# A two-layer graph attention network on one core: another order of work for the last, short node tile

## The chip, the cores and the metric

The kernel runs on one core of one Trainium2 chip. The metric is the device time of one execution, in microseconds (us). Engines go by the profile's names: PE multiplies matrices (PEld is its weight load), DVE and ACT work element by element, POOL issues the gathers, SP and ACT issue plain DMA transfers. PSUM is the memory that PE writes its products into; SBUF is the on-chip memory of everything else.

## The reference

A residual block on 3125 nodes of 768 features with 53,125 directed edges (25,000 drawn pairs in both directions, and a self loop for each node), sorted by destination. Cut to what matters:

```python
h0 = relu(layernorm(x))                                  # no gain, no bias
h = gat(h0, W1, heads=4, out=256, concat)                # 1024 wide
h1 = relu(layer_norm(h, g1, be1)) + h0 @ Wr1 + br1
h = gat(h1, W2, heads=1, out=768)
out = x + layer_norm(h, g2, be2) + h1 @ Wr2 + br2

def gat(h, W, a_src, a_dst, bias):                       # per head
    xl = h @ W
    e = leaky_relu((xl @ a_src)[src] + (xl @ a_dst)[dst], 0.2)
    e = exp(e - segment_max(e, dst)[dst])
    alpha = e / (segment_sum(e, dst)[dst] + 1e-16)
    return segment_sum(xl[src] * alpha, dst) + bias
```

All of it is float32. A graph whose edge list is not in the form above is handled by a second program behind a branch (`any_order`), which does not run here.

## The kernel before

The nodes are cut into NB = 25 tiles of 128 rows, which are the destinations of the sums. The last, tile 24, has only 53 rows (`LAST`). The edges of a tile lie in 17 slots of 128 (`J`), those of tile 24 in 8 (`JL`). A slot covers one or two quarters of a tile's destinations (32 rows each), so the sum of a slot is a matmul whose output is 32 rows: its weights are the attention weights of 128 edges (128 x 32), its moving operand is the 128 gathered source rows. The slots of a tile are taken in five rounds (`ROUNDS`). A float32 matmul shows as two records in the profile.

**Stages.** (1) x is normalised and transposed, and `product(b, i)` (L853 to L872) multiplies each tile by W1 and the folded attention vectors: 1032 columns in three steps of C = 344, six matmuls a step. ACT copies each step out of PSUM into `row`, and the row is stored to `table1` in DRAM (L870); the attention scores go to `asad1`. Beside it runs other work (`beside`), and after each pair of matmul groups the loop takes steps of it. (2) Source scores are looked up for each edge slot, and the layer-1 softmax is made. (3) `sums` (L655) gathers the rows of `table1` by POOL's indirect DMA (L197, L201) and sums them by PE (L757). When a tile's last round is issued, its `finish` is added to a list `running`; every later round takes one step of each member of that list (`step`). `finish` reads the sum out of PSUM (for the first tiles after some rounds of waiting), and goes on into `end1` (L1151 to L1204), which does the bias, the layer norm (L498 statistics, L502 square root on ACT, L1166 normalisation), the transposes on PE (L1173, `flip`), ReLU and gain on ACT (L1178, `turn`), the residual's addition on DVE (L1180), the product with W2 (L1195 by `dense`: L182 for a tile of 128 rows, L186 for one of 53), the copies of that product by ACT (L1201) and DVE (L1203), and the store of the row to `table2` (L218). The products h0 @ Wr1 for some tiles are made in `later`, by the same `pr` buffers in PSUM, which are two, as are the `p2` buffers that transposes and W2 products share. (4) Layer 2 goes through the same tiles: for tile b the five rounds of `summed` (L1379) run while the softmax of tile b + 1 is prepared: `values` (L1322: ACT spreads one gathered column over 32 lanes of `slots`), `softmax` (L1333; transposes into `mix` L1340, maximum L1343, exponentials L1349 and L1350, transposes back L1354, weights copied by DVE L1357 and ACT L1358), `totals2` (L1403 to L1407). `finish` (L1384) adds the tile's own share to the sum in `pa` (L1392), scales it by the softmax's total and adds the bias (L1396), normalises (L1399, L1400) and stores. The product h1 @ Wr2 fills PE between the rounds (`residuals`). `pa` and `mix` have one PSUM buffer each in layer 2.

**`dense`** (L179) is a matmul that for a tile of fewer than 128 rows is cut into pieces of 32 output rows, which take different columns of the array; `half_at` (L188) gives the rows of PSUM for a half of the output columns, so that the two halves of a 53-row tile lie side by side: rows 0 to 52 and 64 to 116.

**What sets the order.** In layer 1's sums and in layer 2 the instructions of PE, ACT and DVE keep the order in which the code issues them (`manual_schedule`); the generators' `yield`s decide it. SP and POOL issue what is left in the order that the framework gives them, each transfer waiting for its buffer and its data. A buffer with a name and a count (`bufs`) is waited for when the same name comes round.

**Names in this text.** `own` is the row of a node itself (its self loop); `v` holds, per node, the sum of exponentials, the self loop's exponential, twice that (v2) and the reciprocal of the total (v3); `xr` is x plus the second residual; `z` is the row that is normalised; `h1` holds a tile's transposed layer-1 result.

## Time and profile before

| What | Value |
|---|---|
| three runs | 1892.24, 1896.75, 1896.78 us |
| median | 1896.75 us |
| profiled execution, own time | 1885.98 us |
| its span | 1884.1 us |
| mean granted clock of PE | 0.966 |
| busy: PE, weight loads, DVE | 1720.1 (91%), 939.4 (50%), 1000.9 us (53%) |
| busy: POOL, ACT | 906.1 (48%), 446.4 us (24%) |
| moved | 541.28 MB, mean 287 GB/s |

The profile is of one execution, and its time lies below the three others. The span runs from the first to the last instruction. In the page's chain of work that ended last, PE has 24% of the span, and DVE, DMA and the rest a few per cent each; the stages are better read one by one. The DMA's row over 40 slices reads 7 and 8 tenths in the first two, 2 to 5 (once 8) until the 11th, 9 from the 12th to the 25th, 4 in the 26th, and 8 to 9 from there to the last but one. The granted clock's row is at 9 almost throughout, with an 8 in the 12th, 27th, 35th and 39th slice and a 7 in the last.

### The profile page before, as it was taken

How to read it: one execution, taken by the hardware profiler on the slowest of the kernel's cores; microseconds unless marked ns; L12 is line 12 of the kernel's file. 1: busy time of each engine (PE TensorE's matmuls, PEld its weight loads, DVE VectorE, ACT ScalarE, POOL GpSimd, SP SyncE). 2: the span in 40 equal slices, each digit the busy share in tenths (PEclk: the TensorE clock that was granted, in tenths of full speed). 3: DMA queues.
4: the chain of work that ended last, by engine and by line, in shares of the span. 5: the costliest groups of instructions: out<-in, count | busy, mean ns of one | idle time of the engine just before them, and what ended most of it. 6: DMA issues, size and time to landing. Idle time of an engine off the chain costs nothing. (4 is left out here: it accounts for less than half of the span.)

```text
span 1884.1 us, 31010 instructions
## 1 busy us (share of the span) xinstructions
PE 1720.1 (91%) x11411; PEld 939.4 (50%) x11411; DVE 1000.9 (53%) x2641; ACT 446.4 (24%) x1286; POOL 906.1 (48%) x922
## 2 busy tenths in 40 slices
PE   8999999999889999999999998969778989889884
PEld 5666665566456555565555544433333334333331
DVE  7673433888845556656655655412434434244435
ACT  2122331000212211221221211222323333233232
POOL 2000102000256666666666666166666666666662
PEclk9999999999989999999999999989999999899987
DMA  7824538432399999999999999499899899999883
GB/s 231 292 83 143 144 88 286 138 129 94 135 383 373 384 384 373 387 368 389 372 367 378 364 362 362 168 373 312 301 323 331 317 328 321 330 335 323 293 295 130
DMA packets 173672, 541.28 MB, mean 287 GB/s; under 512 B 32963, under 2 KB 58329, under 8 KB 173384
## 3 DMA queue, kind: packets, MB, share of 16 engines
q0 software_dynamic: 100912, 381.56, 55.9%
q1 hardware_dynamic: 68206, 147.26, 22.7%
q10 hardware_dynamic: 4394, 10.39, 1.4%
q8 instruction: 93, 1.52, 0.3%
q14 instruction: 67, 0.55, 0.1%
HBM read 498.62 MB, written 65.62 MB: 299 GB/s over the span
## 5 line engine op out<-in xcount | busy, mean ns | idle before, releaser
L197 POOL DMA_INDIRECT g<-table,idx_s x409 | 414.7, 1014 | 406.0 <-DVE al L606 174.8
L201 POOL DMA_INDIRECT g<-table,hi_s x423 | 434.7, 1028 | 239.9 <-issue 88.8
L1379 PE MATMUL pa<-g,w 128*32 128x384 f32 x1956 | 239.4, 520 | 62.7 <-issue 33.2
L182 PE MATMUL pr<-wr,h 128*128 128x384 f32 x768 | 283.0, 508 | 2.1 <-issue 2.1
L757 PE MATMUL pa<-g,w 128*32 128x256 f32 x3912 | 255.8, 387 | 15.7 <-issue 10.1
L182 PE MATMUL p<-w,h1T 128*128 128x384 f32 (+1 forms) x768 | 267.4, 496 | 0.0
L182 PEld LDWEIGHTS pr<-wr,h 128*128 128x128 f32 x768 | 141.4, 196 | 126.5 <-issue 58.5
L182 PEld LDWEIGHTS p<-w,h1T 128*128 128x128 f32 x768 | 139.9, 189 | 113.2 <-issue 21.8
L757 PEld LDWEIGHTS pa<-g,w 128*32 128x32 f32 x3912 | 122.3, 110 | 141.5 <-issue 50.7
L1379 PEld LDWEIGHTS pa<-g,w 128*32 128x32 f32 x1956 | 62.8, 113 | 215.9 <-issue 175.7
L734 DVE TENSOR_TENSOR w<-oh,al 128x128 f32<-128x128 f32 (+1 forms) x416 | 131.9, 317 | 61.5 <-PE pa L757 21.7
L1343 DVE CUSTOM_DVE_ANT_0 e<-mix,pen 128x640 f32<-128x640 f32 x25 | 20.6, 825 | 262.9 <-PE mix L1340 125.8
L182 PE MATMUL pr<-h0k,wr 128*128 128x256 f32 (+1 forms) x576 | 143.9, 395 | 1.1 <-issue 0.9
L862 PE MATMUL pm<-w,h0l 128*128 128x344 f32 (+1 forms) x468 | 142.5, 459 | 0.0
L999 PE MATMUL pm<-h0g,wr 128*128 128x512 f32 x288 | 132.8, 608 | 0.0
L862 PE MATMUL pm<-w,h0g 128*128 128x344 f32 x432 | 130.3, 457 | 0.3 <-ACT h0g L841 0.3
L182 PEld LDWEIGHTS pr<-h0k,wr 128*128 128x128 f32 x576 | 106.7, 192 | 33.2 <-issue 14.4
L930 POOL DMA_DIRECT2D hot_d<-ohd x25 | 13.4, 538 | 221.0 <-DVE own L513 123.7
L733 DVE TENSOR_SCALAR oh<-iota_f,rel_s 128x32 f32<-128x32 f32 (+1 forms) x416 | 114.0, 274 | 0.5 <-issue 0.3
L862 PEld LDWEIGHTS pm<-w,h0l 128*128 128x128 f32 (+1 forms) x468 | 85.7, 187 | 44.9 <-issue 7.1
L862 PEld LDWEIGHTS pm<-w,h0g 128*128 128x128 f32 x432 | 81.6, 192 | 40.5 <-issue 1.2
L1322 ACT ACTIVATE slots<-g 128x32 f32<-128x32 f32 x416 | 66.8, 219 | 131.9 <-DMA g<-table,idx_s 91.1
(288 smaller groups left out, 1671.1 us busy)
## 6 DMA issues: line engine op xcount, KB each, us to landing
s<-slo_d SPq DMA_DIRECT2D x25, 544.0 KB
table<-row SPq DMA_DIRECT2D x24, 512.0 KB
own<-table SPq DMA_DIRECT2D x24, 512.0 KB
h1T_d<-h1T SPq DMA_DIRECT2D x24, 512.0 KB
h<-h1T_d SPq DMA_DIRECT2D x22, 512.0 KB
table<-row SPq DMA_DIRECT2D x24, 392.0 KB
ring<-in_x_dram SPq DMA_DIRECT2D x24, 384.0 KB
xr<-in_x_dram SPq DMA_DIRECT2D x24, 384.0 KB
```

What stands on the lines that cost most here:

```text
L182: nc.tensor.matmul(out_, lhsT, rhs, start=start, stop=stop)
L197: nc.gpsimd.indirect_dma_start(out=g, out_offset=None, in_=table[:, :], in_offset=bass.IndirectOffsetOnAxis(ap=idx_s[:, c], axis=0))
L201: nc.gpsimd.indirect_dma_start(out=g, out_offset=None, in_=table[:, :], in_offset=bass.IndirectOffsetOnAxis(ap=idx_k[:, c], axis=0), bound ...
L733: nc.vector.tensor_scalar(oh, iota_f[:, lo:hi], rel_s[:, c:c + 1], None, op0=OP.is_equal)
L734: nc.vector.tensor_tensor(w, oh[:, None, :].to_broadcast([128, heads, hi - lo]), al[:, POS[j], :, b:b + 1].to_broadcast([128, heads, hi - ...
L757: nc.tensor.matmul(pa[p0:p0 + 32, o // f, o % f:o % f + n], w[:, o // cols, :], g[:, o:o + n], start=to not in opened, stop=False, skip_gr ...
L862: nc.tensor.matmul(pm[:r, :C], h0[b][:, k, :], w1[:, k, i * C:(i + 1) * C], start=(k == 0), stop=(k == NK1 - 1))
L930: nc.gpsimd.dma_start(hot_d[b], ohs[b])
L999: nc.tensor.matmul(pm, wr1[:, k, m * 128:(m + 1) * 128], groups[gi][:, k, :], start=(k == 0), stop=(k == NK1 - 1))
L1322: nc.scalar.activation(slots[b % 2][:, POS[j], :], gs[b, j][:, C2:C2 + 1].to_broadcast([128, 32]), AF.Copy)
L1343: nc.vector.tensor_tensor_reduce(out=e, in0=mix[:, :WIN], in1=pen, scale=1.0, scalar=-BIG, op0=OP.add, op1=OP.max, accum_out=top)
L1379: nc.tensor.matmul(pa[p0:p0 + 32, i, :f], w_, g[:, i * f:(i + 1) * f], start=(i, q) not in opened, stop=False, skip_group_check=True)
```

## The change

It touches the last tile (53 rows) in three places.

**A, `product`.** For the 53-row tile a step of 344 columns is cut into two halves of 172, which `dense` puts side by side: per step and per k four matmuls (two halves, each in pieces of 32 and 21 rows) in place of one of 344 columns. ACT copies each half on its own.

**B, the end of layer 1.** After the last tile's rounds the list `running` is turned round, so that in each step the members of later tiles are taken first: tile 24's `finish` ahead of tile 23's. The last tile's transposes go into a `pr` buffer in place of a `p2` buffer. Tile 23's loop over W2 yields twice more after the sixth of its eight steps.

**C, the end of layer 2.** In tile 23, ahead of its first round, the own rows of tile 24 are loaded, into a buffer of the `h1` kind; the rest of the values of tile 24 are spread and its softmax is begun. The weights and totals of tile 24 follow behind round 1 in place of round 4. A new function, `own_share`, has POOL multiply the own rows by v2 and v3 and add the bias b2 (two instructions). `finish` of tile 24 then computes z = pa * v3 + own, and leaves out the separate scaling and bias. The load of the own rows at the end of tile 23's `finish` is gone.

The diff, cut to its core:

```diff
@@ sums
             k = 0
+            running.reverse()
             while running:
@@ product
+                    parts = 1 if r == P else 2
+                    n = C // parts
                     for k in range(NK1):
-                        nc.tensor.matmul(pm[:r, :C], h0[b][:, k, :], w1[:, k, i * C:(i + 1) * C],
-                                         start=(k == 0), stop=(k == NK1 - 1))
+                        for h in range(parts):
+                            o = i * C + h * n
+                            dense(pm[:, :n], h0[b][:, k, :], w1[:, k, o:o + n], r,
+                                  start=(k == 0), stop=(k == NK1 - 1), at=half_at(b, h).start)
...
+                            for h in range(parts):
+                                o = i * C + h * n
+                                e = min(o + n, HC) - o
+                                at = half_at(b, h)
+                                nc.scalar.activation(row[:, o:o + e], pm[at, :e], AF.Copy)
...
@@ end1
-                    pt = pp.tile([128, 512], F32, name="p2", bufs=2).rearrange("p (k n) -> p k n", n=128)
+                    pt = pp.tile([128, 512], F32, name="pr" if b == NB - 1 else "p2", bufs=2).rearrange("p (k n) -> p k n", n=128)
...
                     if k in (2, 5):
                         yield
+                    if k == 5 and b == NB - 2:
+                        yield
+                        yield
@@ load_own
+                if b == NB - 1 and b not in owns:
+                    owns[b] = small([128, NK2, P], "h1", bufs=3).rearrange("p k n -> p (k n)")[:, :C2]
@@ finish, layer 2
+                if b < NB - 1:
+                    nc.vector.scalar_tensor_tensor(z[:, cs], own[:r, cs], v[:, 2:3], pa[half_at(b, i), i, :f],
+                                                   op0=OP.mult, op1=OP.add)
+                else:
+                    nc.vector.scalar_tensor_tensor(z[:, cs], pa[half_at(b, i), i, :f], v[:, 3:4], own[:r, cs],
+                                                   op0=OP.mult, op1=OP.add)
-            load_own(b + 1)
+            if b + 1 < NB - 1:
+                load_own(b + 1)
             yield
-            nc.vector.scalar_tensor_tensor(z, z, v[:, 3:4], b2_b[:r], op0=OP.mult, op1=OP.add)
+            if b < NB - 1:
+                nc.vector.scalar_tensor_tensor(z, z, v[:, 3:4], b2_b[:r], op0=OP.mult, op1=OP.add)
...
+        def own_share(b):
+            r = rows_of(b)
+            own, v = owns[b][:r], shares[b][1][:r]
+            nc.gpsimd.tensor_scalar(own, own, v[:, 2:3], v[:, 3:4], op0=OP.mult, op1=OP.mult)
+            nc.gpsimd.tensor_tensor(own, own, b2_b[:r], OP.add)
@@ layer 2's loop
+                last = b + 1 == NB - 1
                 for k in range(len(ROUNDS)):
+                    if last and k == 0:
+                        load_own(b + 1)
+                        for i in range(2, len(ROUNDS)):
+                            values(b + 1, i)
+                        made = softmax(b + 1)
+                        next(made)
                     summed(b, k, pa, opened)
...
-                    if b + 1 < NB:
+                    if b + 1 < NB and not last:
...
-                        if b + 1 < NB:
-                            next(made)
-                            next(made, None)
-                            totals2(b + 1)
+                    if b + 1 < NB and k == (1 if last else 4):
+                        next(made)
+                        next(made, None)
+                        totals2(b + 1)
+                        if last:
+                            own_share(b + 1)
```

What this does to the instructions is seen best in rows of the order, where each row is one instruction (or a run of like ones): line, operation, output, inputs, rows x columns. A number behind a name tells buffers apart.

DVE at the end of layer 1, before: rows of 53 are tile 24's, the copy of 128x2 takes tile 23's attention scores out of its W2 product.

```order
L498 BN_AGGR bn_mv<-bn_st 53x2
L1203 COPY asad_109<-p_11999 128x2
L506 RECIPROCAL bn_rs<-bn_sd 53x1
L1166 TENSOR_SCALAR z<-z,bn_mv,bn_rs 53x1024
L1180 TENSOR_TENSOR h1T<-h1T,r1l 128x4x53 x2
L1190 MEMSET row_12066 53x15
```

The same place on DVE now (lines below the first edit are 9 to 12 higher).

```order
L498 BN_AGGR bn_mv<-bn_st 53x2
L506 RECIPROCAL bn_rs<-bn_sd 53x1
L1175 TENSOR_SCALAR z<-z,bn_mv,bn_rs 53x1024
L1189 TENSOR_TENSOR h1T<-h1T,r1l 128x4x53 x2
L1215 COPY asad_109<-p_12056 128x2
L1199 MEMSET row_12123 53x15
```

Tile 23's copy stood between tile 24's statistics and its normalisation; it now stands behind tile 24's residual addition.

PE at the same place, before: the two `p` of 384 and 386 columns are tile 23's W2 product, `ident,z` are tile 24's transposes, and the pieces of 32 and 21 rows are its W2 product.

```order
L182 MATMUL p_11998<-w_4663,h1T 128x384
L182 MATMUL p_11999<-w_4663,h1T 128x386
L182 MATMUL p_11998<-w_4663,h1T 128x384
L182 MATMUL p_11999<-w_4663,h1T 128x386
L1173 MATMUL p_12045<-ident,z 128x53 x4
L1173 MATMUL p_12050<-ident,z 128x53 x4
L186 MATMUL p_12068<-w_4663,h1T 32x384
```

PE at the same place now.

```order
L1182 MATMUL pr<-ident,z 128x53 x8
L182 MATMUL p_12055<-w_4720,h1T 128x384
L182 MATMUL p_12056<-w_4720,h1T 128x386
L182 MATMUL p_12055<-w_4720,h1T 128x384
L182 MATMUL p_12056<-w_4720,h1T 128x386
L186 MATMUL p_12125<-w_4720,h1T 32x384
```

The eight transposes stand ahead of the last two of the eight steps of tile 23's product, and in the `pr` buffers.

ACT at the end of layer 2, before: the exponentials (e, then v) and the copy of 128x128 are of tile 24's softmax, the first store is tile 22's output, the square root of 128x1 is tile 23's.

```order
L1322 ACTIVATE slots_12124<-g_16096 128x32
L1349 ACT_TABLE_LOAD
L1349 ACTIVATE e,v<-e,top 128x640
L1350 ACTIVATE v<-self_s,top 128x1
L218 DMA out_dram<-z 128x768
L1358 ACTIVATE w<-mix 128x128
L502 ACT_TABLE_LOAD
L502 ACTIVATE bn_sd<-bn_mv,eps 128x1
```

The same place on ACT now; the first square root is tile 22's, the second tile 23's.

```order
L1336 ACTIVATE slots_12181<-g_16153 128x32
L1363 ACTIVATE e,v<-e,top 128x640
L1364 ACTIVATE v<-self_s,top 128x1
L502 ACT_TABLE_LOAD
L502 ACTIVATE bn_sd<-bn_mv,eps 128x1
L1372 ACTIVATE w<-mix 128x128
L218 DMA out_dram<-z 128x768
L502 ACTIVATE bn_sd<-bn_mv,eps 128x1
```

Tile 24's exponentials stand ahead of tile 22's square root, without a table load of their own, and the one table load that is left stands ahead of tile 22's square root; tile 23's needs none.

9 lines of the change are left out of this document (3 added, 6 removed).

## The prediction

> **What bounds the kernel now.** I read the table of windows first, because the kernel is a chain of stages with different limits, and then the timelines of all engines at the three places that the change touches: around 294 us, around 1200 us and from 1850 us to the end. Columns of the first fence: window, its length, busy time of PE, its weight loads, DVE, ACT and POOL, granted clock, DMA share, GB/s.
>
> ```profile
> 340.00:380.00 40.00, 40.00 (x367) 25.14 (x366) 35.53 (x77) 2.75 (x4) 0.00 (x0) 0.97 0.34 111
> 700.00:900.00 200.00, 198.94 (x1669) 117.93 (x1668) 122.09 (x401) 40.97 (x117) 132.45 (x132) 1.00 1.00 381
> 1300.00:1500.00 200.00, 170.87 (x950) 72.06 (x950) 78.97 (x164) 63.02 (x199) 131.21 (x131) 0.95 0.90 315
> ```
>
> Between the layers' gathers (340 to 380) PE has no gap and the DMA is two thirds idle: PE bounds it. In layer 1's sums (700 to 900) PE and the DMA are both full. In layer 2 (1300 to 1500) the DMA is at 0.90 and PE at 85%: gathers, PE and a clock a little below 1 share the limit. None of these long stretches is changed. What is changed are the joints between them, and a joint that ends earlier moves everything behind it, if what follows starts from that joint. So the three parts are costed one by one and the rest is taken to shift. (A measurement of this kernel can tell about 0.3%, 5.7 us, from no change.)
>
> **Part 1, the last tile's W1 product.** Timeline rows: start, length, engine, line, operation, operands, count, and in brackets the idle time before it and what ended it.
>
> ```profile
> 293.83 10.62 PE L862 MATMUL pm<-w,h0l 128*53 128x344 f32 x36
> 304.80 0.58 DVE L551 TENSOR_REDUCE own<-pd 128x136 f32<-128x408 f32 x1 [8.77 <-PE pd L545]
> 309.16 1.01 POOL L197 DMA_INDIRECT g<-table,idx_s  x1 [2.58 <-PE pm L999]
> 508.82 4.85 PE L757 MATMUL pa<-g,w 128*32 128x256 f32 x32 [4.04 <-DVE w L734]
> 1130.39 1.93 PE L757 MATMUL pa<-g,w 128*32 128x256 f32 x32
> 1184.00 1.07 PE L757 MATMUL pa<-g,w 128*32 128x256 f32 x16
> 350.33 2.45 PE L562 MATMUL pq<-tabs,ohs 128*128 128x100 bf16 x51
> ```
>
> Removed: 18 matmuls of 344 columns for 53 rows (36 records, two for each float32 matmul), 10.62 us. Added: each becomes four of 172 columns, on 32 (or 21) columns of the array each, so 144 records that can run four abreast, as the sums of L757 do. Their price: 16 more records of L757 cost 1.93 - 1.07 = 0.86 us, 54 ns each at 256 columns, hence 36 ns at 172, and 144 x 36 ns = 5.2 us: 5.4 us saved. The other end: the densest stream of pairs of a weight load and a matmul that this trace has (L562) takes 2.45 / 51 = 48 ns a pair at only 100 columns; if 48 ns is a floor, 144 x 48 = 6.9 us and 3.7 us are saved. I take 4.5, between the two; L757 is the same kind of work, so its end is the nearer one, less something for the denser stream of instructions. The added copies by ACT (two of half the width in place of one) cost nothing: ACT has 2.75 busy us in the window of 40.
>
> A rule of the Trainium skill speaks against this part: "TensorE: Matmul & The Clock Gate", section "Back-to-back issue gap", gives about 81 ns for a pair of weight load and matmul at 128 columns in a sustained stream. By it 144 x 81 ns = 11.7 us, a loss of 1.0 us where the rows give a gain (an estimate from that page). The trace disagrees with it for pairs on a quarter of the array: 54 ns at 256 columns. It is kept as a rival.
>
> Is this on the path? DVE idled 8.77 us until the product was through the queue, and POOL's first gather of layer 1 waits for the rows stored after it. Then PE runs without a gap, and the first sums at 508.82 wait for DVE's weights, which come out of that chain. Nothing in it starts from another event that I can see, so the 4.5 us arrive at 508.82, and since the gathers of layer 1 follow the buffers that the sums release, behind it too.
>
> **Part 2, the end of layer 1.** Rows of PE, DVE, ACT, SP and POOL, then the clock row and a full-speed row of the same matmuls.
>
> ```profile
> 1197.68 10.65 PE L182 MATMUL p<-w,h1T 128*128 128x384 f32 x32
> 1210.11 0.67 PE L1173 MATMUL p<-ident,z 53*128 53x53 f32 x8 [1.77 <-DVE z L1166]
> 1212.29 7.80 PE L186 MATMUL p<-w,h1T 128*32 128x384 f32 x64 [1.51 <-DVE h1T L1180]
> 1204.41 0.20 DVE L498 BATCH_NORM_AGGREGATE bn_mv<-bn_st 53x2 f32<-53x12 f32 x1
> 1208.90 0.16 DVE L1203 COPY asad<-p 128x2 f32<-128x2 f32 x1 [4.29 <-ACT row L1201]
> 1209.16 0.80 DVE L1166 TENSOR_SCALAR z<-z,bn_mv,bn_rs 53x1024 f32<-53x1024 f32 x1
> 1207.77 1.09 ACT L1201 ACTIVATE row<-p 128x384 f32<-128x384 f32 x2 [2.83 <-PE p L182]
> 1210.57 2.41 ACT L1178 ACTIVATE h1T<-p,be_c,g_c 128x53 f32<-128x53 f32 x8 [1.70 <-PE p L1173]
> 1220.66 0.69 SPq L218 DMA_DIRECT2D table<-row  x2
> 1223.76 1.00 POOL L197 DMA_INDIRECT g<-table,idx_s  x1 [38.20 <-DMA hot<-hot_d]
> 1213.10:1216.40 3.30, 3.30 (x26) 1.07 (x28) 0.30 (x2) 0.00 (x0) 0.00 (x0) 0.50 0.31 66
> 1833.16 2.78 PE L186 MATMUL pr<-wr,h 128*32 128x384 f32 x32
> ```
>
> The last tile's statistics are done at 1204.41, but its normalisation waits until 1209.16: ahead of it on DVE stands tile 23's copy L1203, which waits for ACT's row copy, which waits for the end of tile 23's W2 product. Now the copy stands behind the chain. On PE the eight transposes now stand ahead of the product's last quarter, and in another PSUM buffer, so they need not wait for its release. New times: six of eight steps of the product end at 1197.68 + 24 x 0.333 = 1205.7; the normalisation, free from about 1205.0, ends at 1206.0; transposes to 1206.7; the last eight records to 1209.3. ACT turns the tile (2.41 us) from 1206.5 to 1208.9 beside that, DVE's additions end by 1209.4. The last tile's W2 product then waits only for ACT's copies of tile 23 out of the same two buffers (1.09 us, to 1210.4): it starts near 1210.1. Its 64 records took 7.80 us because the clock row shows 0.50 for 3.3 us of them; at the full-speed row they take 2 x 2.78 = 5.6. With idle time down from 3.3 to under 1 us the clock should stay up: end at 1215.7 instead of 1220.1. I take 4.0 saved; 4.5 if nothing is lost in hand-overs, 1.5 if the clock falls all the same and the row buffer is late. That buffer is single: tile 24's row must wait until tile 23's is stored, now about 1210.5 plus the 3.1 us that a store took here until the first gather (1220.66 to 1223.76), 1213.6, so 2 us ahead of need. SP stores in the new order too, h1T of tile 24 ahead of tile 23's row, and loses nothing. POOL's first gather of layer 2 follows the last row's store, so layer 2 shifts by 4.0.
>
> **Part 3, the end of layer 2.** Rows of DVE, ACT, then PE, then the closing chain.
>
> ```profile
> 1850.74 1.14 DVE L1392 SCALAR_TENSOR_TENSOR z<-own,v,pa 128x384 f32<-128x384 f32 x2 [3.06 <-remote]
> 1851.80 0.68 DVE L1357 COPY w<-mix 128x512 f32<-128x512 f32 x1
> 1852.69 0.69 ACT L1322 ACTIVATE slots<-g 128x32 f32<-128x32 f32 x5
> 1855.44 0.45 ACT L1322 ACTIVATE slots<-g 128x32 f32<-128x32 f32 x3
> 1862.28 0.83 ACT L1349 ACTIVATE e<-e,top 128x640 f32<-128x640 f32 x1 [5.08 <-DVE e L1347]
> 1852.54 6.85 PE L1379 MATMUL pa<-g,w 128*32 128x384 f32 x48 [5.12 <-DVE v L1405]
> 1859.32 0.77 PE L1340 MATMUL mix<-ident,slots 128*128 128x128 f32 x5
> 1860.02 2.79 PE L1379 MATMUL pa<-g,w 128*32 128x384 f32 x32
> 1865.99 3.42 PE L1379 MATMUL pa<-g,w 128*32 128x384 f32 x36 [1.97 <-DVE v L1405]
> 1864.20 1.13 DVE L1392 SCALAR_TENSOR_TENSOR z<-own,v,pa 128x384 f32<-128x384 f32 x2
> 1868.71 1.28 ACT L502 ACT_TABLE_LOAD   x1 [2.47 <-DVE bn_mv L498]
> 1866.34 0.99 DVE L1396 SCALAR_TENSOR_TENSOR z<-z,v,b_b 128x768 f32<-128x768 f32 x1
> 1872.38 1.23 DVE L1392 SCALAR_TENSOR_TENSOR z<-own,v,pa 53x384 f32<-53x384 f32 x2
> 1873.65 1.01 DVE L1396 SCALAR_TENSOR_TENSOR z<-z,v,b_b 53x768 f32<-53x768 f32 x1
> 1877.47 1.01 DVE L1400 SCALAR_TENSOR_TENSOR z<-z,bn_rs,xr 53x768 f32<-53x768 f32 x1
> ```
>
> Tile 23's sums are the 80 records from 1852.54 on, with tile 24's softmax in between; tile 24's are the 36 at 1865.99, but the end is DVE's chain: from 1864.20 to 1878.48. On ACT the exponential stands behind the previous tile's with no square root between, so its table load is gone, and the square root's comes before tile 22's statistics, where ACT waits anyway: tile 23's finds its table there.
>
> What it adds: PE must transpose all eight slots of tile 24 before tile 23's first round. ACT copies eight from 1852.7 at 0.14 us each, to 1853.8; all rows had landed by 1855.44 at the latest, since the last three copies then waited for nothing. So PE starts at 1853.9 (at worst 1855.9), 0.77 us of transposes at full clock and twice that here, and the rounds begin at 1855.4 instead of 1852.54. The 48 records of 6.85 us ran at half clock until 1858.2 (2.79 / 32 = 87 ns at full clock, 174 at half): 16 records until then, 16 more to 1859.6, five transposes to 1860.3, the remaining 48 x 87 ns = 4.2 us to 1864.5. The softmax needs 0.77 + 3.0 us from its first transposes to its exponential (1859.32 to 1863.11), to about 1858.5, under the first two rounds. Before, the rounds ended at 1862.81, but DVE reached L1392 only at 1864.20; now 1864.5. So 0.3 us are lost ahead of the chain. In it go tile 24's weight copy and totals (1865.33 to 1866.34, 1.0), the table load that tile 23's square root waited for (1.28), and L1396 of the last tile (1.0): 3.3. Net 3.0. Tile 24's sums (3.42 us) cannot start before L1392 has freed their buffer, 1865.7, and end at 1869.1, 1 us ahead of DVE. POOL's two operations on the own rows are not in this trace as POOL work; DVE takes 1.01 for one like them. They can start near 1861.5 and are wanted at 1870.4: nothing at up to four times DVE's time, and beyond that a delay of the excess. SP loads the own rows much earlier, in a buffer freed by the residual of tile 22, ahead of nothing that waits. Bounds: 3.5 saved, or 0, if the rows land late or the 3.06 us that DVE spent before 1850.74 for a releaser that the profile cannot name were an accident: without it the old order would have started sooner and the new one not.
>
> **The sum.** -4.5 - 4.0 - 3.0 = -11.5 us. The profiled execution took 1885.98 us, of which its span is 1884.1; the sum gives 1874.5 for a like one. The median of the three runs is 1896.75, 10.8 above it, and nothing in the change touches what differs there, so 1896.75 - 11.5 = 1885.2.
>
> **The rivals.**
>
> ```profile
> 1821.89 1.52 PE L186 MATMUL pr<-wr,h 128*32 128x384 f32 x3 [0.73 <-issue]
> 1437.00:1459.50 22.50, 19.82 (x122) 8.65 (x122) 10.14 (x21) 7.40 (x25) 16.07 (x16) 1.00 0.93 341
> 1459.50:1489.50 30.00, 26.24 (x122) 10.04 (x122) 10.12 (x21) 9.52 (x27) 19.19 (x19) 0.89 0.88 316
> ```
>
> Rival 1, the short matmuls starve. Around 1822 the same kind of matmul came at about 0.75 us each, waiting for nothing that the profile names. Ten such pairs in the burst of 144 would take back the 5.4 us: gain 11.5 - 4.5 = 7.0, 1889.8. For: the burst needs 288 instructions in 5 us while W1's successor is being loaded. Against: layer 1's sums run as densely. Chance 0.13. "Runtime: NRT & Kernel Launch" of the Trainium skill, section "Instruction fetch mechanics", says instructions arrive in blocks of 256 and that crossing a block is mostly hidden; by it this rival is void, and the row above is why I keep it.
>
> Rival 2, the floor for a pair: if 144 pairs take longer than the 10.62 us they replace, part 1 loses 1.0: -6.0, 1890.8. Against: 54 ns. Chance 0.04. (This is the section on the back-to-back gap, cited above.)
>
> Rival 3, the shift is swallowed: layer 1's sums have the DMA at 1.00, and if its transfers and not the sums' start set their end, part 1 is gone; with part 3 at its bound of 0 only part 2 remains: -4.0, 1892.8. Chance 0.13.
>
> Rival 4, slower. Two tiles of layer 2 with the same 122 matmuls took 22.5 us at clock 1.00 and 30.0 at 0.89: a dip of the clock costs 7.5 us a tile. Where the dips fall depends on when PE waits. If the shifted instruction stream brings three more such tiles, 3 x 7.5 - 11.5 = +11.0, 1907.8; from two and a half on it is slower by over 0.3%. For: dips are frequent. Against: the matmuls and gathers of tiles 0 to 22 are unchanged in number and order, and a dip less is as likely as one more. Chance 0.07.
>
> **How the numbers follow.** The forecast has 0.63: 1885, between 1881 and 1890 by its own bounds. The range of 1877 to 1893 adds the runs' own spread of 4.5 us below and rivals 1 to 3 above, and leaves out rival 4 and the tails. Faster by over 0.3% means below 1891.1: the forecast, most of rivals 1 and half of 2, 0.75. Within 0.3%: rival 3 and what is left, 0.18. Slower: 0.07.
>
> **What would show it.** Part 1: the 144 records in 5 to 7 us, and the first sums near 504. Part 2: the normalisation of 53x1024 right behind its statistics, the last W2 product at clock 1.00 in under 6 us, the first gather of layer 2 about 8.5 us earlier than before. Part 3: no table load between tile 23's statistics and its square root, POOL's two operations ended before DVE's first of tile 24, and 11 us in place of 14.3 from tile 23's L1407 to the end of DVE. I am wrong if the first sums do not move with the product, if the clock is again 0.50 in the last W2 product, or if tile 23's rounds wait for a gather.

## The result, and the profile after

Over 21 runs of each, the changed kernel took 1879.07 us in the median (1872.97 to 1897.23), the kernel before 1895.54 (1883.98 to 1904.32): a ratio of 0.9918 with a 95% interval of 0.9899 to 0.9937. By that ratio it is 15.5 us less, between 11.9 and 19.1 (the two medians lie 16.5 apart). The forecast was 11.5 less, 1885 us, with a range of 1877 to 1893. The profiled execution of the changed kernel took 1879.73 us with a span of 1877.9, at a granted clock of 0.974 (0.966 before).

I go by the same three joints. First the timeline of the changed kernel around tile 24's W1 product (start, length, engine, line, operation, operands, count, and in brackets the idle time before it with what ended it).

```profile
291.62 5.45 PE L186 MATMUL pm<-w,h0l 128*32 128x172 f32 x144
297.23 5.38 PE L1008 MATMUL pm<-h0g,wr 128*128 128x512 f32 x12
297.43 0.58 DVE L551 TENSOR_REDUCE own<-pd 128x136 f32<-128x408 f32 x1 [3.60 <-PE pd L545]
301.88 1.01 POOL L197 DMA_INDIRECT g<-table,idx_s  x1 [2.67 <-PE pm L1008]
500.32 4.72 PE L757 MATMUL pa<-g,w 128*32 128x256 f32 x32 [4.04 <-DVE w L734]
```

The product takes 5.45 us in place of 10.62: 38 ns for each of 144 records. DVE's wait for it has gone from 8.77 to 3.60 us, and the first sums start at 500.32 in place of 508.82. Of these 8.5 us, 2.2 were there before the edited product began (at 291.62 in place of 293.83), and the edit has no part in them; counted from the product's start, the first sums come 208.70 us behind in place of 214.99.

The timeline at the end of layer 1, and behind it the row of the windows' table for the last W2 product (window, its length, busy time of PE, weight loads, DVE, ACT and POOL, granted clock, DMA share, GB/s).

```profile
1206.57 0.20 DVE L498 BATCH_NORM_AGGREGATE bn_mv<-bn_st 53x2 f32<-53x12 f32 x1
1207.33 0.80 DVE L1175 TENSOR_SCALAR z<-z,bn_mv,bn_rs 53x1024 f32<-53x1024 f32 x1
1208.19 0.70 PE L1182 MATMUL pr<-ident,z 53*128 53x53 f32 x8 [0.28 <-DVE z L1175]
1208.82 2.86 PE L182 MATMUL p<-w,h1T 128*128 128x384 f32 x8
1211.65 6.18 PE L186 MATMUL p<-w,h1T 128*32 128x384 f32 x64
1217.26 0.07 DVE L1199 MEMSET row<- 53x15 f32 x1 [4.87 <-DMA table<-row]
1217.32 1.06 ACT L1213 ACTIVATE row<-p 53x384 f32<-53x384 f32 x2 [5.11 <-PE p L186]
1221.48 1.00 POOL L197 DMA_INDIRECT g<-table,idx_s  x1 [34.61 <-DMA hot<-hot_d]
```

```profile
1211.65:1217.80 6.15, 6.15 (x66) 1.96 (x65) 0.23 (x2) 0.98 (x2) 0.00 (x0) 1.00 0.37 103
```

The normalisation stands 0.76 us behind its statistics (4.75 before), the transposes run while tile 23's product is under way, and tile 24's W2 product runs at a clock of 1.00. From the statistics to the first gather of layer 2 it is 14.91 us in place of 19.35. But note the first row: the statistics come at 1206.57, later than before (1204.41), though the sums began 8.5 us earlier. That had to be explained before anything else could be believed.

The timeline at the end of layer 2:

```profile
1847.52 1.13 DVE L1407 SCALAR_TENSOR_TENSOR z<-own,v,pa 128x384 f32<-128x384 f32 x2
1849.46 1.04 ACT L1336 ACTIVATE slots<-g 128x32 f32<-128x32 f32 x8
1850.21 1.33 PE L1354 MATMUL mix<-ident,slots 128*128 128x128 f32 x5 [2.31 <-ACT slots L1336]
1851.47 5.13 PE L1393 MATMUL pa<-g,w 128*32 128x384 f32 x32
1858.62 1.73 POOL L1432 TENSOR_SCALAR h<-h,v 53x768 f32<-53x768 f32 x1 [16.48 <-DVE v L1427]
1859.52 1.63 DVE L1420 SCALAR_TENSOR_TENSOR z<-z,bn_rs,xr 128x768 f32<-128x768 f32 x1
1860.43 2.39 POOL L1433 TENSOR_TENSOR h<-h,b_b 53x768 f32<-53x768 f32 x1
1861.37 1.14 DVE L1407 SCALAR_TENSOR_TENSOR z<-own,v,pa 128x384 f32<-128x384 f32 x2 [0.23 <-PE pa L1393]
1865.02 0.29 ACT L502 ACTIVATE bn_sd<-bn_mv,eps 128x1 f32<-128x1 f32 x1 [6.69 <-DVE bn_mv L498]
1867.40 1.26 DVE L1410 SCALAR_TENSOR_TENSOR z<-pa,v,h 53x384 f32<-53x384 f32 x2
1871.35 1.01 DVE L1420 SCALAR_TENSOR_TENSOR z<-z,bn_rs,xr 53x768 f32<-53x768 f32 x1
```

Tile 23's square root at 1865.02 has no table load ahead of it, and from tile 23's L1407 at 1861.37 to the end of DVE at 1872.36 it is 10.99 us (14.28 before). From tile 22's sum on (1847.52, before 1850.74) it is 24.84 us in place of 27.74.

### The profile page after: what moved, and what is told of

Same layout as the page of the kernel before. It is cut to its first block, busy times and chain, and to the rows that moved or that the text cites. A ratio compares the mean times of both kernels' runs of the same rounds, so it can differ in the third digit from the quotient of the medians.

```text
span 1877.9 us, 31229 instructions
## 1 busy us (share of the span) xinstructions
PE 1725.0 (92%) x11519; PEld 939.4 (50%) x11519; DVE 998.8 (53%) x2640; ACT 444.5 (24%) x1287; POOL 913.6 (49%) x924
## 4 chain that ended last, share of the span: by engine, by line
PE 80%; DVE 7%; issue 6%; DMA 4%; another core or an unknown queue 2%; POOL 1%; ACT 0%; SPq 0%; POOLq 0%; DVEq 0%; ACTq 0%
PE pr L182 19%; PE p L182 13%; PE pa L757 12%; PE pm L182 11%; PE pa L1393 11%; PE pm L1008 5%; PE pq L562 3%; DMA g<-table,idx_s 2%; PE p L1182 1%; PE mix L1354 1%; DMA w<-in_L_gnn_W_dram 1%; POOL g L197 1%; PE mix L1368 1%; PE pt L840 1%
## 5 line engine op out<-in xcount | busy, mean ns | idle before, releaser
L1393 PE MATMUL pa<-g,w 128*32 128x384 f32 x1956 | 243.4, 506 | 54.6 <-issue 49.4
L757 PE MATMUL pa<-g,w 128*32 128x256 f32 x3912 | 265.3, 387 | 17.4 <-issue 11.4
L757 PEld LDWEIGHTS pa<-g,w 128*32 128x32 f32 x3912 | 121.7, 110 | 154.7 <-issue 67.7
L182 PE MATMUL pm<-w,h0l 128*128 128x344 f32 x432 | 130.2, 455 | 0.0
L182 PEld LDWEIGHTS pm<-w,h0l 128*128 128x128 f32 x432 | 80.3, 190 | 38.6 <-issue 0.2
L1336 ACT ACTIVATE slots<-g 128x32 f32<-128x32 f32 x416 | 67.0, 220 | 137.3 <-DMA g<-table,idx_s 89.8
```

Of the source, the lines that this page charges most:

```text
L182: nc.tensor.matmul(out_, lhsT, rhs, start=start, stop=stop)
L757: nc.tensor.matmul(pa[p0:p0 + 32, o // f, o % f:o % f + n], w[:, o // cols, :], g[:, o:o + n], start=to not in opened, stop=False, skip_gr ...
L1336: nc.scalar.activation(slots[b % 2][:, POS[j], :], gs[b, j][:, C2:C2 + 1].to_broadcast([128, 32]), AF.Copy)
L1393: nc.tensor.matmul(pa[p0:p0 + 32, i, :f], w_, g[:, i * f:(i + 1) * f], start=(i, q) not in opened, stop=False, skip_group_check=True)
```

## The experiments

My theory going in: the three joints give 5.2, 4.4 and 2.9 us, each passes through to the end, and the late statistics are scatter between executions. The first rival: the sums' end is set by transfers, so part A is swallowed. Each group of experiments ran on one chip beside runs of the kernel before. Two levels of time appeared: in the first group the kernel before took 1784.89 us, in the two others 1901.23 and 1891.63. The two slower groups ran on one and the same chip and the first group on another, so I call them the slower and the faster chip; whether it is the chip or a condition of it, the runs don't tell. The chip of the first measurement is not on record; its time is that of the slower one. Only ratios within a group are compared.

**The kernel before once more.**

> The kernel before, unchanged, profiled once more. The layer-1 sums, from PE's first sum to tile 24's statistics, took 695.6 us in the profile of before and 706.3 in the profile of the changed kernel, so the 8.5 us that the first sums came earlier were gone at their end. My theory: the length of this stretch varies from execution to execution whatever the kernel, and the profile of before caught a short one (its own 1885.98 us lie 9.6 below the median of 1895.54): here the stretch comes out between 699 and 710 with an own time of 1890 to 1900. Rival (the shift is swallowed): the end of the stretch is set by transfers and not by its start; then the old kernel has the stretch at 695 to 697 again, with statistics near 1204. Ratio to before 1.000 within 0.003 by both.

Ratio 0.9997 (0.9985 to 1.0009). It ran on the faster chip, where the sums' stretch took 671.5 us, so neither number could come out. The question was settled by the stretches of all profiles together, in the table below.

**Part A alone** (twice, with the edit of part A only).

> Part A alone: tile 24's W1 product in halves side by side, all else as before. My theory: the product takes 5.4 us as in the changed kernel (10.6 before), the first sums come 5 to 8 us earlier, the sums' stretch is as long as in the unchanged kernel of this call within its scatter of some 10 us, and the time falls by 5.2 to 8.5 us: ratio 0.9955 to 0.9973. Rival (swallowed): the stretch is longer by what the start came earlier, ratio 0.999 to 1.001. Second rival (more than its own size): the new phase of the instruction stream takes stalls out of later stages, ratio below 0.994.

> Part A alone once more. My theory: its shift passes through on either chip, ratio 0.996 to 0.998. Rival (the slower chip swallows the shift, as the first pair of traces looked): 0.999 to 1.001 where the time before is about 1895.

Faster chip: 0.9967 (0.9953 to 0.9982), 5.9 us less. Its first sums came at 500.91, 5.1 us earlier than in the unchanged kernel beside it (506.01). The rows of A, and below them those of the unchanged kernel:

```profile
295.13 5.45 PE L186 MATMUL pm<-w,h0l 128*32 128x172 f32 x144
500.91 4.68 PE L757 MATMUL pa<-g,w 128*32 128x256 f32 x32 [4.04 <-DVE w L734]
```

```profile
293.88 10.61 PE L862 MATMUL pm<-w,h0l 128*53 128x344 f32 x36
506.01 4.67 PE L757 MATMUL pa<-g,w 128*32 128x256 f32 x32 [4.04 <-DVE w L734]
```

Slower chip: 0.9998 (0.9972 to 1.0025), which is the rival's number, with 5.2 us less just at the interval's edge. Its profile shows the product at its new length and the first sums at 502.25, and every stretch behind it of the usual length, so the profile does not support the rival, but the runs do not show the gain either. What is shown on both chips is that the shorter product reaches the first sums: counted from the product's start, they come 208.7 to 209.3 us behind in the five profiles of the slower chip that have part A, and 212.5 to 216.2 in the five that don't; on the faster chip 205.8 in A against 212.1 and 212.2.

**The double cost of A:** tile 24's W1 product three times, in the kernel before.

```diff
+                    if r < P:
+                        for k in 2 * list(range(NK1)):
+                            nc.tensor.matmul(pm[:r, :C], h0[b][:, k, :], w1[:, k, i * C:(i + 1) * C],
+                                             start=(k == 0), stop=(k == NK1 - 1))
                     for k in range(NK1):
```

> The kernel before with tile 24's W1 product made three times (two more products of 10.6 us, each overwritten by the next): the start of what follows is delayed by 21.2 us. My theory: the delay passes through whole, 19 to 23 us, ratio 1.010 to 1.012. Rival (swallowed): the transfers of layer 1 keep their own pace and give back part of it, ratio under 1.005.

1.0096 (1.0077 to 1.0114), 13.7 to 20.3 us more, a little under the 19 to 23 that I expected. In the profile the first sums start 21.5 us later than in the unchanged kernel (527.48 against 506.01), the stretch is as long (670.4 against 671.5), and DVE ends 21.5 us later (1799.86 against 1778.40); the profiled execution is the longest of its six. So most of the delay passes through, by the runs about 17 of 21 us, by the profile all of it. The rival (under 1.005) falls on this chip.

**B and C without A.**

> The change without part A: the ends of both layers as in the changed kernel, the W1 product as before. My theory: the gains at the joints read in the two traces, 4.4 us from tile 24's statistics to the first gather of layer 2 and 2.9 us from tile 22's sum to the end of DVE, add up: 7.3 us less, ratio 0.995 to 0.997. Rival (A brings nothing): the whole of the measured change, ratio 0.992, stands here.

1.0005 (0.9993 to 1.0017): a miss for both. At the joint the 4.1 us were there (14.92 against 18.98), at the end of layer 2 they were not. The timeline of that kernel there:

```profile
1753.57 0.67 PE L1346 MATMUL mix<-ident,slots 128*128 128x128 f32 x3 [2.07 <-ACT slots L1328]
1755.29 0.52 ACT L1328 ACTIVATE slots<-g 128x32 f32<-128x32 f32 x2 [1.65 <-DMA g<-table,idx_s]
1755.85 0.69 PE L1346 MATMUL mix<-ident,slots 128*128 128x128 f32 x2 [1.61 <-ACT slots L1328]
1756.47 4.85 PE L1385 MATMUL pa<-g,w 128*32 128x384 f32 x32
1766.09 1.14 DVE L1399 SCALAR_TENSOR_TENSOR z<-own,v,pa 128x384 f32<-128x384 f32 x2 [0.23 <-PE pa L1385]
```

And the unchanged kernel beside it:

```profile
1753.44 1.14 DVE L1392 SCALAR_TENSOR_TENSOR z<-own,v,pa 128x384 f32<-128x384 f32 x2 [0.51 <-PE pa L1379]
1755.24 4.08 PE L1379 MATMUL pa<-g,w 128*32 128x384 f32 x48 [1.18 <-DVE v L1405]
1764.12 1.13 DVE L1392 SCALAR_TENSOR_TENSOR z<-own,v,pa 128x384 f32<-128x384 f32 x2
```

PE wants tile 24's slots ahead of tile 23's rounds, ACT waits 1.65 us for tile 24's last gathers until 1755.29, and the rounds start at 1756.47. This is the sign that the prediction had named for being wrong: tile 23's rounds wait for a gather. Tile 22's sum to tile 23's takes 15.2 us (1750.88 to 1766.09) where the unchanged kernel takes 10.7: 4.5 us, more than the 3.3 that the closing chain has gained. Of the 4.5 us, the gather's wait is 1.65. Another 2.1 are the new order itself: where nothing is waited for (all profiles of C on the slower chip that begin the softmax ahead of the first round), the rounds begin 3.94 us behind tile 22's sum in place of 1.80. The rest, 0.7, comes from the rounds: PE's first 32 records take 4.85 us at a granted clock of 0.69, read over the 8 us from tile 22's sum.

The other two old-order profiles of this chip (A, and A's product thrice) take 11.9 and 12.4 us from sum to sum, because there ACT waits for the last gathers too, but behind three of the five rounds. With their ends of 26.2 and 26.6 us beside the 25.0 of the unchanged kernel, the 26.2 of B and C is no loss, and no gain. The three profiles in which ACT waited can be compared from the end of ACT's last copy on: to DVE's last instruction it is 18.9 us in both of the old order and 21.3 in the new one. So where the last gather set the pace, C cost 2.4 us, by the one profile that shows it.

On the slower chip the same move costs almost nothing: no gather is waited for, and the old order's rounds are slow anyway. There the first 48 records of the old order's rounds take 5.4 to 6.9 us, at a clock of 0.57 to 0.79 over the same 8 us; on the faster chip they take 4.08 at 1.00 in all three profiles. From sum to sum the new order takes 12.9 us in the mean of four profiles against 12.7 in four of the old one, so its later start is hidden; on the faster chip there was nothing to hide it behind.

Of the 4.1 us at the joint, layer 2's stretch ahead of that had already taken 2.9 (559.9 against 557.0); one profile does not tell whether that is scatter (a stretch of 555.3 is among the four of this chip). But from the first gather of layer 2 to the end of ACT's last copy it is 564.8 us, against 562.6 and 565.2 in the two old-order profiles in which ACT waited, so the joint's gain did reach the last gather.

How far ahead the gathers are on each chip stands in the groups of PE's lines from 1260 to 1690 us, here for the unchanged kernel on the faster chip (count, busy time and mean ns, idle time before it with its releasers):

```profile
L1379 PE MATMUL pa<-g,w 128*32 128x384 f32 x1520 | 145.5, 501 | 0.0
L1340 PE MATMUL mix<-ident,slots 128*128 128x128 f32 x95 | 17.6, 326 | 45.1 <-ACT slots L1322 45.1
```

and in the first profile of before:

```profile
L1379 PE MATMUL pa<-g,w 128*32 128x384 f32 x1328 | 160.7, 514 | 41.9 <-issue 24.9 <-DVE w L1357 9.1 <-DVE v L1405 6.8
L1340 PE MATMUL mix<-ident,slots 128*128 128x128 f32 x85 | 13.6, 285 | 7.0 <-issue 7.0
```

On the faster chip PE waits only for slots, that is for gathers, which run at 363 GB/s with the DMA at 0.98: each gather is used as soon as it lands. On the slower chip (322 GB/s, 0.92) PE waits mostly for nothing that the profile names, and the gathers are ahead of it. An order that asks for the last gather one step earlier waits for nothing there.

**The changed kernel beside its parts, on the slower chip** (twice).

> The changed kernel itself, beside its parts. On the chip where the kernel before took 1785 us the gathers are faster (the sums' stretch 671 us against 696 to 706), part A alone gave 0.9967 and parts B and C together 1.0005. My theory now: what B and C bring at their joints depends on whether tile 24's last gather has landed when PE wants it; where it lands late (as in that run of B and C, where PE waited for ACT's slots, ACT for the gather until 1755.29) they bring nothing. Then here, if the time before is again about 1785: ratio 0.996 to 0.998, A's gain alone. Rival (the parts act together: what A brings forward, B and C then keep): ratio 0.990 to 0.994, as first measured. If the time before is about 1895, both expect 0.990 to 0.994.

> The changed kernel once more, beside three other kernels. Two chips have been met: on one the kernel before takes about 1785 us and its layer-2 sums show 3.2 us of PE idle without a releaser, on the other 1895 to 1901 us with 50 to 68 us of it. My theory: on the faster one the change is worth A alone, ratio 0.996 to 0.998, on the slower one all three joints, 0.991 to 0.995. Rival: the change is worth the same on both, 0.991 to 0.995.

0.9942 (0.9919 to 0.9965), 11.0 us less, and 0.9925 (0.9897 to 0.9952), 14.2 less. Both agree with the forecast and with the first measurement. The whole change was not run on the faster chip, so its worth there can only be put together from its parts: A's 5.9 and nothing from B and C.

**B alone and C alone.**

> Part B alone: tile 24's end of layer 1 ahead of tile 23's. The joint from tile 24's statistics to the first gather of layer 2 shortens by 4 us by both theories (19.0 in the unchanged kernel, 14.9 with B and C). My theory: layer 2 is paced by its gathers from the first to the last, so the last gather lands 4 us earlier too, and the old end of layer 2 follows it: 3 to 5 us less, ratio 0.9972 to 0.9983. Rival (layer 2 gives the shift back on the way): the last gather is issued at the same time as in the unchanged kernel, ratio 0.999 to 1.001.

> Part C alone: tile 24's softmax ahead of tile 23's rounds. My theory: PE's first round of tile 23 must wait for tile 24's last gather, which lands about 1 us after the old order would have started that round; the waiting costs what the shorter chain saves: from the end of the last gather's transfer to DVE's last instruction 21.8 us as with B and C (20.2 in the unchanged kernel), ratio 1.000 to 1.002. Rival (C is worth 2.9 us as in the first pair of traces): ratio 0.998 to 0.999.

B: 0.999 (0.9971 to 1.0009), 5.5 less to 1.7 more; its joint took 14.90 us. The ratio is the rival's, but the runs can't tell the 4.3 us of the joint from none, so they decide between theory and rival no more than B and C together did. C: 0.9966 (0.9943 to 0.9989), 2.1 to 10.8 less. My expectation for C (1.000 to 1.002) came from the faster chip and failed on this one; the rival's 0.998 to 0.999 lies at the interval's edge. In the profile ACT copied all eight slots without a gap (the row L1336 x8 above, and the like in this run), and the end from tile 22's sum took 23.5 us.

**The softmax one round later,** against that wait.

```diff
-                    if last and k == 0:
+                    if last and k == 1:
...
-                    if b + 1 < NB and k == (1 if last else 4):
+                    if b + 1 < NB and k == (2 if last else 4):
```

> The changed kernel with tile 24's softmax begun ahead of round 1 of tile 23 in place of round 0, and ended behind round 2 in place of round 1. My theory: one round (16 matmul records a half, about 2.8 us) stands between tile 24's last gather and its transposes, so PE no longer waits for the gather, and the shorter chain's gain is kept: 1 to 3 us less than the changed kernel of this call where gathers land late, the same within 1 us where they land early. Rival (the gathers' end sets the end whatever the order): no difference to the changed kernel.

0.9963 (0.9945 to 0.9982), 7.0 us less, against the whole change's 0.9942 in the same group; the two intervals overlap. The expected 1 us of sameness was wrong where the profile can tell: the end from tile 22's sum takes 26.5 us against 23.8 in the changed kernel beside it. Its timeline:

```profile
1872.06 0.68 DVE L1371 COPY w<-mix 128x512 f32<-128x512 f32 x1
1873.18 1.14 DVE L1407 SCALAR_TENSOR_TENSOR z<-own,v,pa 128x384 f32<-128x384 f32 x2
1874.36 2.69 DVE L1416 SCALAR_TENSOR_TENSOR z<-z,v,b_b 128x768 f32<-128x768 f32 x1
1874.40 1.82 POOL L1433 TENSOR_TENSOR h<-h,b_b 53x768 f32<-53x768 f32 x1
```

Tile 24's weight copy is back in DVE's chain ahead of tile 23's sum, and POOL's addition now meets DVE's L1416, which takes 2.69 us in place of the 1.00 that it takes for tile 22 in this kernel. It was not tried on the faster chip, for which it was made.

**C without the own share on POOL.**

```diff
-                        if last:
-                            own_share(b + 1)
```

(against part C alone, and with the old two lines of `finish` for tile 24)

> Part C without the own share on POOL: tile 24's softmax, weights and totals ahead as in the changed kernel, but its finish is the old one (own row times v2 plus sum, then scaling and bias on DVE). My theory: the chain from tile 23's sum to the end of DVE is 11.6 to 12.0 us, 1.0 for the scaling that is back, against 11.0 with the whole of part C and 14.3 before; DVE's last step of tile 23 takes 1.0 in place of 1.6, since POOL is idle. Rival (POOL's work is what made room): 13.5 to 14.3 us.

1.0014 (0.999 to 1.0039). The timeline:

```profile
1870.67 1.02 DVE L1403 SCALAR_TENSOR_TENSOR z<-z,bn_rs,xr 128x768 f32<-128x768 f32 x1
1872.52 1.14 DVE L1394 SCALAR_TENSOR_TENSOR z<-own,v,pa 128x384 f32<-128x384 f32 x2 [0.83 <-PE pa L1381]
1879.75 1.01 DVE L1399 SCALAR_TENSOR_TENSOR z<-z,v,b_b 53x768 f32<-53x768 f32 x1
1883.57 1.01 DVE L1403 SCALAR_TENSOR_TENSOR z<-z,bn_rs,xr 53x768 f32<-53x768 f32 x1
```

From tile 23's sum to the end it is 12.06 us, 1.07 more than with the whole of C and just above the expected 11.6 to 12.0, and DVE's last step of tile 23 takes 1.02 in place of 1.63. So of the 3.3 us that the closing chain lost, POOL's share is 1.1 and the order 2.2. The runs' ratio is worse than C's by more than that (9 us, with intervals of 4 to 5 on either side); the profiles show nothing for the difference.

**The double cost of B:** tile 24's W2 product three times, in the kernel before.

```diff
-                for k in range(NK2):
+                for k in (3 if b == NB - 1 else 1) * list(range(NK2)):
```

> The kernel before with tile 24's W2 product made three times: the first gather of layer 2 is delayed by two more products, 11 to 16 us as the profile will show. My theory: layer 2 is paced from its first gather, so the time grows by the delay, ratio 1.006 to 1.009. Rival (layer 2 gives a shift of its start back, which would be why part B alone brought only 0.999): ratio 1.000 to 1.004.

1.010 (1.0062 to 1.0138), 11.7 to 26.1 us more. The product took 17.95 us in place of 7.8, so the delay was 10.1 (less than I had put), the joint 29.49 us. Layer 2 behind it took 627.8 us, no less than in other profiles: a shift of its start is not given back. The runs lost more than the delay. Part of that goes with the granted clock: the mean over its six executions is 0.960, against 0.965 for the kernel before, and among the kernel before's own executions in the three groups 0.01 less clock goes with 8 to 10 us more time. By that (an estimate from these runs) about 4 us of the loss go with the clock. The means of the executions lie 16.0 us apart, so some 12 are left, near the delay of 10.1. Whether the clock makes the time or the same thing makes both, the runs don't tell.

**All profiles by stages,** each boundary read from the timeline: "sums" from the first sums of L757 to tile 24's statistics, "joint" from there to the first gather of layer 2, "layer 2" from there to tile 22's sum, "end" from there to DVE's last instruction.

| chip | kernel | first sums at | sums | joint | layer 2 | end |
|---|---|---|---|---|---|---|
| slower | before | 508.8 | 695.6 | 19.4 | 627.0 | 27.7 |
| slower | changed | 500.3 | 706.3 | 14.9 | 626.0 | 24.8 |
| slower | changed, beside its parts | 501.4 | 705.1 | 14.9 | 645.5 | 23.8 |
| slower | changed, once more | 501.5 | 699.3 | 14.9 | 625.7 | 23.5 |
| slower | B | 509.7 | 710.2 | 14.9 | 633.4 | 26.3 |
| slower | C | 505.8 | 705.4 | 19.3 | 642.0 | 23.5 |
| slower | softmax later | 504.1 | 705.6 | 14.9 | 634.6 | 26.5 |
| slower | A | 502.3 | 703.2 | 20.3 | 625.7 | 27.0 |
| slower | C without POOL | 510.7 | 701.1 | 20.3 | 626.7 | 25.7 |
| slower | B's product thrice | 508.2 | 703.5 | 29.5 | 627.8 | 26.7 |
| faster | before | 506.0 | 671.5 | 19.0 | 557.0 | 25.0 |
| faster | A | 500.9 | 672.0 | 18.4 | 555.3 | 26.2 |
| faster | A's product thrice | 527.5 | 670.4 | 17.9 | 557.5 | 26.6 |
| faster | B and C | 504.2 | 671.9 | 14.9 | 559.9 | 26.2 |

The joint takes 14.9 us in every profile with B and 17.9 to 20.3 in those without it (leaving out the product made thrice). The end on the slower chip takes 23.5 to 24.8 us with C in the changed order and 26.3 to 27.7 without C; on the faster chip it is 26.2 with C and 25.0 to 26.6 without. The long stretches scatter on the slower chip by 15 us (sums) and 20 us (layer 2), with no relation to the edits that I can see: the same changed kernel has 645.5 and 625.7. Layer 2's length goes roughly with its granted clock: from 1260 to 1690 us the four profiles above 630 us have 0.90 to 0.93, the six below it 0.93 to 0.97. The first profile of before has the shortest sums of all, 9 us under the mean of the other nine (704.4). That fits its execution of 1885.98 us, where the median is 1895.54, and it is why the first pair of traces looked as if the sums had swallowed part A. The faster chip's four stretches of sums lie within 2 us of each other, with the first sums between 500.9 and 527.5, so there that reading is refuted. On the slower chip the five profiles with A have sums of 703.9 us in the mean and the five without 703.2, which does not support it, but with a scatter of 15 us does not exclude it either.

## Why the prediction was right, point by point

**What bounds the kernel.** Right in that a joint which ends earlier moves what follows. Not seen: that the limit of layer 2 changes from chip to chip between gathers and PE. One of its readings is off without weight in the sum: the window from 340 to 380 lies ahead of layer 1's sums, which start at 508.82, and not between the two layers' gathers.

**Part 1, predicted 4.5 (3.7 to 5.4 by the rows).** The product saved 10.62 - 5.45 = 5.2 us. The row of L757 gave 36 ns a record, and 38 were measured; the 48 ns of L562, taken as a possible floor, is none for these narrower records, and moving away from the nearer row cost accuracy. Here the two halves lie side by side, so that two half-width matmuls take the place of one, and 10.62 / 5.45 = 1.95. The Trainium skill, "TensorEngine Tiling (Array Packing)", section "Theoretical Speedup", gives up to 2 times for a small dimension of at most 64; the trace agrees, with 53 rows and 1.95. Rival 1 (starving) did not come: the 144 records stand in the trace without a gap. (Its price was loose: at about 0.75 us each, some eight such pairs would take back 5.4 us, not ten.) Rival 2 (a floor for a pair, by which the product would have become longer than 10.62 us) did not either.

**Part 2, predicted 4.0 (1.5 to 4.5).** 4.4 in the first pair, 14.9 against a mean of 19.2 in the others without B: 4.3. Every step of it is in the rows above. Two sizes were off and cancelled, which is luck: the last W2 product took 6.18 us, not 5.6, but began 5.1 us behind the statistics, not 5.7. The size that was off by most is the store of tile 23's row, put at 3.1 us: the buffer came free at 1217.26, 5.0 us after the store's issue at 1212.23. It is wanted by ACT's copy of the product at 1217.32, so 0.06 us were left and not 2. In the five other profiles with B the store took 3.4 to 4.8 us and left 0.3 to 1.7; the joint was 14.9 each time, but the margin that the prediction counted on was hardly there. The first gather of layer 2, named as a sign at 8.5 us earlier, came 2.3 earlier in that pair, since the short sums of the first profile hid the rest.

**Part 3, predicted 3.0 (0 to 3.5).** 2.9 in the first pair; in the profiles of the slower chip 23.9 (four with the whole of C in the changed order) against 26.9 (four without C): 3.0. The chain of 11 us was 10.99, and the 0.3 us to be lost ahead of it are the 12.9 against 12.7 of the sum-to-sum times on the slower chip. The lower bound, 0, "if the rows land late", is what the faster chip showed; but late rows are only part of the reason. The 0.3 had as a premise that the old order's rounds run at half clock anyway, as they did in the profile of before (6.85 us for 48 records), and on the faster chip they ran at full clock (4.08). "POOL's two operations cost nothing" came out so in time only: they held up DVE's L1420 by 0.6 us, which a wait for PE covered.

**The sum.** 5.2 + 4.3 + 3.0 = 12.5 by the profiles, between the 11.0, 14.2 and 15.5 that the runs gave for the whole, and inside all three intervals. The parts measured alone on the slower chip add up to 0.4 + 1.9 + 6.5 = 8.8, with 4 to 5 us of uncertainty on each, so the runs do not divide the gain; the stages do. That part A's 5.2 us reach the end is measured on the faster chip; on the slower one, where the whole change was measured, it is inferred from the whole and the stages. What the runs gave beyond 12.5 is not assigned to anything.

**Rival 3 (swallowed)** falls on the faster chip, by A alone, A's product thrice and the table. On the slower chip it is not supported, and A alone, at 0.9998, has not refuted it. **Rival 4 (three more tiles at a low clock in layer 2)** has its size in the table, 20 us between profiles, and the longer ones do have the lower clock; but it comes as scatter of the same kernel and not as an effect of the change.

## What to carry to other kernels

Price an edit at a joint from the joint's own rows, and look at the stretches between only to see that they do not change: a whole span of one execution can hide an 8 us gain behind 10 us of scatter. An order that uses the last transfer one step earlier is only free while transfers are ahead of their use; find out which side of that line the kernel is on before the reorder, since it can change with the chip. A cost that hides behind a stretch at low clock, as the later start of tile 23's rounds did, is hidden only while that stretch is slow. Small matmuls with few output rows belong side by side on the array, priced by rows of the same form.

## What the runs showed of the hardware

The same program with the same bytes took 1785 us in one group and 1892 to 1901 in others: from 1260 to 1690 us the gathers ran at 363 against 322 GB/s, and in the two groups quoted above PE had no idle time without a releaser, against 31.9 us (24.9 and 7.0) on the slower chip. What holds PE's instructions up there was not tried.

The clock that PE was granted around the end of layer 2 differs between the two chips for the same instructions: 48 records of tile 23's rounds took 4.08 us in three profiles (clock 1.00 over the 8 us from tile 22's sum) and 5.4 to 6.9 in four (0.57 to 0.79).

POOL and DVE held each other up. DVE's L1416 took 2.69 us beside POOL's addition of 1.82 us, and 1.00 without it; and POOL's addition took 2.39 and 1.82 us in two kernels. The Trainium skill, "SBUF — State Buffer", section "SBUF: two separate sides", says that a DVE operation with two SBUF inputs and a POOL operation that reads SBUF take one pair of ports as a lock, held for the whole instruction. The rows agree to within 0.13 us: 1.00 + 1.82 is 2.82, and 2.69 was measured.
